# Two buffers for the residual rows of a conditioned transformer block, loaded and biased one block ahead, with a weight ring of eight

## The chip, the cores and the metric

The kernel runs on one core of one Trainium2 chip. The metric is the time of one execution in device microseconds (us); lower is better. All tensors are fp32. The engines that the text names are PE (TensorE, which multiplies matrices), DVE (VectorE), ACT (ScalarE), POOL (GpSimd) and SP (SyncE), whose queue issues nearly all transfers between the chip's main memory and the on-chip memory.

## The reference

The inputs are x with shape [8, 1024, 512], a condition vector [8, 512] and the weights of one block with 16 heads. Cut to what matters, this is computed:

```python
mod = silu(condition) @ Wada + bada
sh_a, sc_a, gt_a, sh_m, sc_m, gt_m = split(mod, 6, axis=1)
xm = layernorm(x, g1, be1) * (1 + sc_a[:, None]) + sh_a[:, None]
x = x + gt_a[:, None] * (causal_attention(xm, Wqkv) @ Wproj + bproj)
xm = layernorm(x, g2, be2) * (1 + sc_m[:, None]) + sh_m[:, None]
h = gelu(xm @ W1 + b1)
x = x + gt_m[:, None] * (h @ W2 + b2)
```

The gates multiply biases too: `gt_a * bproj` and `gt_m * b2` are the same for every token of a batch row, and the kernel adds each to the residual rows as one "bias row".

## The kernel before

The 8 x 1024 tokens are cut into 16 blocks of 512 tokens, two to a batch row; a block's tokens are four tiles of 128 rows. For each block the kernel projects k, q and v, attends, projects out (`proj`), normalizes again (`mt`), and runs the MLP as four up steps (`u`, L1058) and four down steps (`d`, L1107). The k, q, v, up and down products are one level of Strassen's scheme: seven products in place of eight, of operands that are sums of quarters. The sums of weights are made in the first blocks and kept in main memory.

The program is a fixed order of instructions, written by a planner in the kernel itself. It keeps a running estimate of each engine's time in `now`, and of when each value will have been written or released in `written` and `left`. Two streams are interleaved: attention (`attend`, L1743) and the linear work (`plan`, L231, a list of steps for each window). Window `w` holds what runs beside the attention of block `w`: late MLP steps of block `w - 2`, the projection and MLP of block `w - 1`, and the k, q and v of later blocks. Each step is a generator: it yields the values that it needs next, and `work` (L1343) advances the thread with the shortest wait. `start` (L1324) opens a side thread.

Weights come in pieces of 256 KB through a ring of `RING` buffers, in an order that is fixed ahead (`order`, L317). `fetch` (L328) issues the next piece's load on SP as soon as the planner has released a buffer, so in the SP queue the load of piece i + 9 stands right after the place at which piece i was last used, and it waits for PE to get there. SP issues in order. A transfer that has to wait holds up every load behind it.

Four other kinds of transfer stand in the same queue and matter here:

- `store` (L1100) writes a block's finished rows, in two halves. It is recorded right after the last additions to those rows were recorded, so SP waits there until POOL or DVE has done them.
- `load_xr` (L1258) fetches the residual rows of a block: four transfers of 256 KB. There is one buffer (`xrp`, L78), which the block before has to have stored first; block 14 alone borrows a buffer of k. The step stands in the window just ahead of `rows` and `proj`.
- `hat_a<-held_a` (L678) is the second half of a transposition of the next block's normalized input through main memory: four strided loads of 256 KB each.
- `gate_broadcasts` (L508) loads a gate row and a bias row for a batch row, each spread over 128 partitions.

`project_out` (L1006) multiplies the attention output with four pieces of Wproj for each of the four tiles, and POOL or DVE adds the bias row `gba` and the gated product to the residual rows. `down` (L1107) adds `gbm` at its first step. `either` (L150) picks POOL or DVE for such an addition by the planner's times.

Of the kernel before, what the change touches and what calls it, by code (L numbers as in the profile page):

```python
# [9 lines left out]
F32 = mybir.dt.float32  # L10
# [12 lines left out]
def kernel(  # L23
# [47 lines left out]
    HB = D // 2  # L71
    RING = 9

# [154 lines left out]
    def mlp_steps(n):  # L228
# [6 lines left out]
        0: [("load_xa", 2), ("preps",), ("k", 1), ("norm_a", 2), ("gates", "a"), ("q", 1)]  # L235
        + [("mod", 3), ("at", 2), ("v", 1), ("mod", 4), ("columns_m",), ("gates", "m")],
    }
    late = []
    for w in range(1, NB):
        n = w - 1  # L240
        m = mlp_steps(n)
        even = blocks[n][1] == 0
        rows_a = [("rows", blocks[n][0], "a")] if even else []
        rows_m = [("rows", blocks[n][0], "m")] if even else []
        own = m[:1] + ([("load_xa", w + 2)] if w + 2 < NB else []) + m[1:3]
        own += [("norm_a", w + 2)] if w + 2 < NB else []
        if w == NB - 1:
            steps = late[:1] + [("load_xr", n)] + rows_a + [("proj", n), ("mt", n)] + late[1:]
            steps += [("v", w)] + rows_m + own + m[3:6]
            late = m[6:]  # L250
        else:

            steps = late + [("v", w), ("load_xr", n)] + rows_a + [("proj", n), ("mt", n), ("k", w + 1)]
            if w == 2:
                steps = late + [("v", w), ("k", w + 1), ("load_xr", n)] + rows_a + [("proj", n), ("mt", n)]
            if w == 1:
                steps = [("load_xr", n)] + rows_a + [("k", w + 1), ("proj", n), ("mt", n)]
# [11 lines left out]
    plan[NB] = [("load_xr", n), late[0], ("beside", late[1]), ("proj", n), ("mt", n)] + mlp_steps(n)  # L269

# [126 lines left out]
    make_identity(nc, ident)  # L397
    mask = const.tile([P, 2 * P], F32, tag="mask", name="mask")
    for i in range(2):
        make_causal_mask(nc, mask[:, ts(i, P)], MASKED)  # L400
    eps = const.tile([P, 1], F32, tag="eps", name="eps")
    nc.gpsimd.memset(eps, EPS)
    ones = const.tile([P, P], F32, tag="ones", name="ones")
    nc.gpsimd.memset(ones, 1.0)
# [103 lines left out]
    def gate_broadcasts(b, kind):  # L508

        for name in (f"g{kind}", f"gb{kind}"):  # L510
            row = rowp.tile([P, D], F32, tag=f"row{name}", name=f"row_{name}_{b}")
            nc.sync.dma_start(row, kept_rows[name][b : b + 1, :].to_broadcast([P, D]))
            gate_rows[name] = row

# [476 lines left out]

    residual, stored = {}, {}
    y_count, y_keys = [0], {}
# [12 lines left out]
    def project_out(n):  # L1006
        at = take(NC)
        yield [("attended", n)], []
        attT = qTs[n]
        tiles = [residual[n][:, t, :] for t in range(NTT)]  # L1010
        for t, xt in enumerate(tiles):
            xt_job = lambda t=t, xt=xt: add_to(xt, gate_rows["gba"], [("row", "gba")], [("xr", n, t)])
            pool_jobs.append((xt_job, [("xr", n, t)]))
        last = n == NB - 1
# [38 lines left out]
        release(*at)  # L1053
        run_pool_jobs(True)
        if not last:
            normalize(residual[n], f"m{n}", [("xr", n, t) for t in range(NTT)])
# [35 lines left out]
    def settle(n, f, t, y, ky):  # L1092
# [5 lines left out]
        add_to(residual[n][:, half(t, 2), c], y, [ky], keys)  # L1098

    def store(n, t):  # L1100
        b, h = blocks[n]
        for i in (2 * t, 2 * t + 1):
            r0 = h * TB + i * P
            nc.sync.dma_start(out[b, r0 : r0 + P, :], residual[n][:, i, :])
        stored[n + 1] = max(stored.get(n + 1, 0.0), due([("xr", n, 2 * t), ("xr", n, 2 * t + 1)]))

    def down(n, part):  # L1107
# [85 lines left out]
        if part == 0:  # L1193
            yield [("g", n, 0), ("g", n, 1), "prepared"], []
            for i in range(NTT):
                add_to(residual[n][:, i, :], gate_rows["gbm"], [("row", "gbm")], [("xr", n, i)])
            combine(nc.vector, "B12", "B12", "B11")
# [47 lines left out]
    def perform(step):  # L1245
# [12 lines left out]
        elif kind == "load_xr":  # L1258
            n = step[1]
            b, h = blocks[n]  # L1260
            if n == NB - 2:
                xr = kvp.tile([P, NTT, D], F32, tag="kT", name=f"xr_{n}")
            else:
                xr = xrp.tile([P, NTT, D], F32, tag="xr", name=f"xr_{n}")
            residual[n] = xr
            for t in range(NTT):
                r0 = h * TB + t * P
                nc.sync.dma_start(xr[:, t, :], x[b, r0 : r0 + P, :])
                landed = max(now["PE"], stored.get(n, 0.0)) + LANDING + 700 * t
                written["xr", n, t] = landed  # L1270
        elif kind == "norm_a":
# [179 lines left out]
    def diagonals(parts, sc):  # L1451

        if parts[-1][4] == parts[0][4]:
            first, span = parts[0][3] - P, len(parts) * P
            return span, sc[:, :, first : first + span]
        return 2 * P, sc.rearrange("p j (a c) -> p j a c", c=2 * P)[:, :, :, P:]
# [19 lines left out]
    def scores_by_heads(n, g, parts, reads):  # L1476

        h = blocks[n][1]
        for some in (range(HPG - 1), range(HPG - 1, HPG)):
# [14 lines left out]
            for j, bank in of.items():  # L1494
                if parts[0][1] == h:
                    span, place = diagonals(parts, banks[bank].unsqueeze(1))
                    place = place[:, 0]
                    shape_of = mask[:, :span]
                    if len(place.shape) == 3:
                        shape_of = shape_of.rearrange("p (a c) -> p a c", c=P)  # L1500
                    nc.vector.tensor_tensor(place, place, shape_of, ALU.add)
# [8 lines left out]
    def scores_at_once(n, g, parts, reads):  # L1510
# [15 lines left out]
        if parts[0][1] == h:  # L1526
            span, place = diagonals(parts, sc)
            shape_of = mask[:, :span].unsqueeze(1)
            if len(place.shape) == 4:
                shape_of = shape_of.rearrange("p o (a c) -> p o a c", c=P)  # L1530
            nc.vector.tensor_tensor(place, place, shape_of.to_broadcast(place.shape), ALU.add)  # L1531
            note("DVE", 165 + 4.16 * span, ["st"])
# [127 lines left out]
    def finish(n, g):  # L1660
# [7 lines left out]
        for i, (c0, w, term, held) in enumerate(terms):  # L1668
            for j in range(HPG):
                r = slice(j * hd, (j + 1) * hd)  # L1670
                nc.tensor.matmul(  # L1671
                    banks[bank][r, TB - w :], ones[:, :hd], term[:, j, c0 : c0 + w],
                    start=i == 0, stop=i == len(terms) - 1, skip_group_check=True,
# [163 lines left out]
    for n in range(NB):  # L1837
        written["attended", n] = NEVER
        written["v done", n] = NEVER
        written["m used", n] = NEVER  # L1840
        if n > 1:
# [73 lines left out]
```

## Time and profile before

| what | value |
|---|---|
| median of 3 runs | 3567.45 us (3565.46 to 3569.86) |
| the profiled execution's own time | 3568.64 us |
| its span, first to last instruction | 3566.9 us |
| PE busy | 3490.9 us (98%) |
| DVE busy | 2181.1 us (61%) |
| POOL busy | 2081.8 us (58%) |
| ACT busy | 1186.3 us (33%) |
| moved by DMA | 461.77 MB, mean 129 GB/s |
| mean granted clock of TensorE | 0.995 |

The profile page gives the busy time of each engine, the chain of work that ended last, and groups of instructions. A row of a group ends with the engine's idle time just before these instructions and with what ended that idle time. The view of waits sums those idle times by who waited for whom; "SPq" there is SP's queue. The timeline lists instructions in order of time: start, length, engine, line, what is written and read, a count, and in brackets the idle time ahead of them with what ended it.

### The profile page before, as it was taken

The numbers are of one execution on the slowest core, as the hardware profiler recorded it, in microseconds if no ns is written. First come the engines' busy times: TensorE is split into PE (matmuls) and PEld (weight loads), VectorE is DVE, ScalarE is ACT, GpSimd is POOL, SyncE is SP. The second block draws the span as 40 slices with busy tenths as digits, with TensorE's granted clock in tenths as the row PEclk, the third lists the DMA queues.
The fourth block names the chain that finished last, engine by engine and source line by source line (L and its number), as shares of the span: only waits on it lengthen the run. The fifth ranks groups of instructions, "written<-read, shape, count | busy, mean of one in ns | idle before, by whom it ended". The sixth has DMA issues, their size and how long they took to land.

```text
span 3566.9 us, 120690 instructions
## 1 busy us (share of the span) xinstructions
PE 3490.9 (98%) x54621; PEld 1741.5 (49%) x54621; DVE 2181.1 (61%) x2395; ACT 1186.3 (33%) x1229; POOL 2081.8 (58%) x2247
## 2 busy tenths in 40 slices
PE   8999999999999999999999999999999999999999
PEld 4444445444554545445454454544545445454445
DVE  6776575665746557365574665746666466665663
ACT  2334333352323514234241442323423134231521
POOL 3667746675456754577536675366762667526660
PEclk9999999999999999999999999999999999999999
DMA  6753434435453344533445334453344533434334
GB/s 201 241 179 93 141 102 127 124 108 155 113 150 107 104 154 117 158 100 101 146 121 148 105 102 146 120 151 103 103 140 126 152 103 105 143 108 142 92 111 137
DMA packets 318259, 461.77 MB, mean 129 GB/s; under 512 B 27052, under 2 KB 177388, under 8 KB 315700
## 3 DMA queue, kind: packets, MB, share of 16 engines
q1 hardware_dynamic: 317632, 454.03, 43.4%
q8 instruction: 430, 7.05, 0.8%
q14 instruction: 81, 0.66, 0.1%
q10 hardware_dynamic: 116, 0.03, 0.0%
HBM read 408.80 MB, written 43.06 MB: 127 GB/s over the span
## 4 chain that ended last, share of the span: by engine, by line
PE 88%; DMA 4%; POOL 3%; DVE 3%; ACT 1%; issue 1%; SPq 1%; ACTq 0%; DVEq 0%; POOLq 0%
PE bank L202 60%; PE sc L1517 8%; PE po L1650 7%; PE st L1610 7%; PE st L1598 3%; DMA w<-in_L_cond_Wproj_dram 2%; PE bank L1671 2%; POOL pT L1740 1%; DMA hat_a<-held_a 1%; PE bank L728 1%; DVE mx L1534 1%; POOL hT L161 1%; PE bank L1572 0%; DVE sc L1531 0%; DMA w<-in_L_cond_Wada_dram 0%
## 5 line engine op out<-in xcount | busy, mean ns | idle before, releaser
L1740 POOL TENSOR_TENSOR pT<-pT,pT 128x256 f32<-128x256 f32 (+3 forms) x1254 | 1213.2, 1003 | 336.1 <-PE po L1650 183.4
L1622 ACT ACTIVATE pT<-st 128x2048 f32<-128x2048 f32 x288 | 541.0, 1878 | 1115.0 <-PE st L1610 1032.9
L202 PE MATMUL bank<-w,hT 128*32 128x256 f32 x14336 | 813.7, 380 | 0.2 <-POOL pT L1627 0.2
L1534 DVE TENSOR_REDUCE mx<-sc 128x4 f32<-128x2048 f32 (+3 forms) x384 | 666.0, 1755 | 216.2 <-PE sc L1517 210.0
L202 PEld LDWEIGHTS bank<-w,hT 128*32 128x32 f32 x14336 | 451.6, 110 | 367.6 <-issue 82.5
L202 PE MATMUL bank<-xm_m,w 128*32 128x256 f32 x8192 | 498.4, 380 | 0.0
L202 PE MATMUL bank<-t_m,w 128*32 128x256 f32 x6144 | 383.2, 380 | 0.1
L202 PEld LDWEIGHTS bank<-xm_m,w 128*32 128x32 f32 x8192 | 256.0, 110 | 222.2 <-issue 55.5
L1627 POOL TENSOR_SCALAR_AFFINE_SELECT pT<-pT 128x512 f32<-128x512 f32 x256 | 169.0, 678 | 332.4 <-ACT pT L1622 332.2
L1517 PE MATMUL sc<-kT,qT 32*128 32x512 f32 (+3 forms) x3072 | 329.1, 520 | 2.0 <-DVE mx L1534 1.7
L1531 DVE TENSOR_TENSOR sc<-sc,mask 128x1024 f32<-128x1024 f32 (+1 forms) x160 | 162.8, 1018 | 273.5 <-PE sc L1517 187.3
L1650 PE MATMUL po<-pT,v 128*32 128x512 f32 (+3 forms) x3048 | 303.1, 493 | 2.0 <-POOL pT L1627 2.0
L1610 PE MATMUL st<-qT,kT 32*128 32x512 f32 (+3 forms) x3072 | 300.6, 487 | 0.0
L202 PEld LDWEIGHTS bank<-t_m,w 128*32 128x32 f32 x6144 | 189.4, 110 | 180.7 <-issue 57.5
L202 PE MATMUL bank<-w,qT 128*32 128x512 f32 x2048 | 244.7, 606 | 21.2 <-DMA w<-in_L_cond_Wproj_dram 19.7
L1689 DVE RECIPROCAL rec<-rec 128x128 f32<-128x128 f32 x256 | 224.5, 919 | 33.2 <-ACT rec L1680 33.2
L202 PE MATMUL bank<-xm_a,w 128*32 128x256 f32 x3968 | 244.6, 380 | 0.0
L1517 PEld LDWEIGHTS sc<-kT,qT 32*128 32x128 f32 x3072 | 129.3, 183 | 172.8 <-ACT pT L1622 63.9
L202 PE MATMUL bank<-t_a,w 128*32 128x256 f32 x2944 | 190.9, 382 | 0.4 <-ACT xm_m L738 0.4
L193 DVE TENSOR_TENSOR hT<-bank,u_u 128x512 f32<-128x512 f32 x192 | 129.3, 685 | 101.2 <-PE bank L202 99.9
L1064 ACT ACTIVATE hT<-hT,cols 128x512 f32<-128x512 f32 x256 | 164.5, 711 | 55.3 <-DVE hT L193 54.7
L202 PEld LDWEIGHTS bank<-xm_a,w 128*32 128x32 f32 x3968 | 123.5, 110 | 106.5 <-issue 30.8
(216 smaller groups left out, 3396.6 us busy)
## 6 DMA issues: line engine op xcount, KB each, us to landing
w<-in_L_cond_W_dram SPq DMA_DIRECT2D x384, 256.0 KB
w<-kept_up_S SPq DMA_DIRECT2D x256, 256.0 KB
w<-kept_down_S SPq DMA_DIRECT2D x256, 256.0 KB
w<-kept_qkv_S SPq DMA_DIRECT2D x180, 256.0 KB
w<-in_L_cond_Wqkv_dram SPq DMA_DIRECT2D x147, 256.0 KB
hat_a<-in_x_dram SPq DMA_DIRECT2D x64, 256.0 KB
w<-in_L_cond_Wproj_dram SPq DMA_DIRECT2D x64, 256.0 KB
xr<-in_x_dram SPq DMA_DIRECT2D x64, 256.0 KB
```

The source lines that it names most:

```text
L193: nc.vector.tensor_tensor(out, src, other, op)
L202: nc.tensor.matmul(ps[r, :], columns, rhs, start=start, stop=stop, skip_group_check=True)
L1064: nc.scalar.activation(hT[:, i, :], hT[:, i, :], AF.Gelu, bias=cols[:, O_B1 + f : O_B1 + f + 1])
L1517: nc.tensor.matmul(sc[:, j, c0 : c0 + w], qTs[n][r, gg, ts(qt, P)], keys_of(n, kh)[r, gg, :w], start=True, stop=True, skip_group_check=True,)
L1531: nc.vector.tensor_tensor(place, place, shape_of.to_broadcast(place.shape), ALU.add)
L1534: nc.vector.tensor_reduce(maxima[n, gg][:, kh, qt, :], sc[:, :, c0 : c0 + w], axis=AX.X, op=ALU.max)
L1610: nc.tensor.matmul(st[:, j, c0 : c0 + w], kT[r, gg, ts(k % NTT, P)], qT[r, gg, TB - w :], start=False, stop=True, skip_group_check=True,)
L1622: nc.scalar.activation(pT[:, :, :used], st[:, :, :used], AF.Exp, scale=scale)
L1627: nc.gpsimd.affine_select(diagonal, diagonal, pattern=[[0, HPG], [1, P]], compare_op=ALU.is_ge, fill=0.0, base=0, channel_multiplier=-1,)
L1650: nc.tensor.matmul(po[r, TB - w :], v[:, k % NTT, g * P + j * hd : g * P + (j + 1) * hd], pT[:, j, c0 : c0 + w], start=(k == 0), stop=last ...
L1689: nc.vector.reciprocal(some, some)
L1740: nc.gpsimd.tensor_tensor(into, into, pT[:, j, c0 : c0 + w], ALU.add)
```

## The change

- The residual rows get two buffers. `load_xr` becomes a side thread: it waits until the planner thinks block `n - 2` is stored, issues the load as two transfers of 512 KB, waits until the planner has the additions to block `n - 1` that were recorded by then, loads the bias row, and hands the four bias additions to POOL's list of jobs. The step moves from just ahead of `proj` of block `n` to the MLP of block `n - 1`, between its first and second down step. `project_out` no longer adds the bias. Block 14 has a residual buffer like the others.
- The two bias rows share one buffer (`rowgb`). So each is loaded once per block, 16 times each, where each was loaded once per batch row, 8 times. `gbm` is loaded at the end of `project_out`.
- `store` becomes a side thread: it is recorded when the planner thinks the additions are done, and writes two tiles in one transfer.
- The weight ring goes from nine buffers to eight.
- The causal mask is kept for 128 columns and repeated by its access pattern; the tile of ones has 32 columns in place of 128.

```diff
-    RING = 9
+    RING = 8
-    xrp = ctx.enter_context(tc.tile_pool(name="xrp", bufs=1))
+    xrp = ctx.enter_context(tc.tile_pool(name="xrp", bufs=2))
...
-        + [("mod", 3), ("at", 2), ("v", 1), ("mod", 4), ("columns_m",), ("gates", "m")],
+        + [("mod", 3), ("at", 2), ("v", 1), ("load_xr", 0), ("mod", 4), ("columns_m",), ("gates", "m")],
...
-            steps = late + [("v", w), ("load_xr", n)] + rows_a + [("proj", n), ("mt", n), ("k", w + 1)]
+            steps = late + [("v", w)] + rows_a + [("proj", n), ("mt", n), ("k", w + 1)]
...
-                steps += m[3:5]
+                steps += m[3:5] + [("load_xr", w)]
...
-                steps += m[3:6] + at
+                steps += m[3:5] + [("load_xr", w)] + m[5:6] + at
...
+    def bias_row(n, kind):
+
+        b = blocks[n][0]
+        row = rowp.tile([P, D], F32, tag="rowgb", name=f"row_gb{kind}_{n}")
+        nc.sync.dma_start(row, kept_rows[f"gb{kind}"][b : b + 1, :].to_broadcast([P, D]))
+        gate_rows[f"gb{kind}"] = row
+        written["row", f"gb{kind}", n] = now["PE"] + LANDING
...
     def project_out(n):
         at = take(NC)
-        yield [("attended", n)], []
+        yield [("attended", n), ("xr begun", n)], []
...
-        for t, xt in enumerate(tiles):
-            xt_job = lambda t=t, xt=xt: add_to(xt, gate_rows["gba"], [("row", "gba")], [("xr", n, t)])
-            pool_jobs.append((xt_job, [("xr", n, t)]))
...
     def store(n, t):
-        b, h = blocks[n]
-        for i in (2 * t, 2 * t + 1):
-            r0 = h * TB + i * P
-            nc.sync.dma_start(out[b, r0 : r0 + P, :], residual[n][:, i, :])
-        stored[n + 1] = max(stored.get(n + 1, 0.0), due([("xr", n, 2 * t), ("xr", n, 2 * t + 1)]))
+        unstored.setdefault(n, 2)
+
+        def when_added():
+            yield [("xr", n, 2 * t), ("xr", n, 2 * t + 1)], []
+            nc.sync.dma_start(some_rows(out, n, t), residual[n][:, half(t, 2), :])
+            unstored[n] -= 1
+            if unstored[n] == 0:
+                written["stored", n] = now["PE"]
+
+        start(when_added())
+
+    def load_xr(n):
+
+        if n > 1:
+            yield [("stored", n - 2)], []
+        xr = xrp.tile([P, NTT, D], F32, tag="xr", name=f"xr_{n}")
+        residual[n] = xr
+        for t in range(2):
+            nc.sync.dma_start(xr[:, half(t, 2), :], some_rows(x, n, t))
+        for t in range(NTT):
+            written["xr", n, t] = now["PE"] + LANDING
+        if n > 0:
+            yield [("xr", n - 1, t) for t in range(NTT)], []
+        bias_row(n, "a")
+        row = ("row", "gba", n)
+        for t in range(NTT):
+            job = lambda t=t: add_to(xr[:, t, :], gate_rows["gba"], [row], [("xr", n, t)])
+            pool_jobs.append((job, [("xr", n, t), row]))
+        written["xr begun", n] = 0.0
...
-            yield [("g", n, 0), ("g", n, 1), "prepared"], []
+            yield [("g", n, 0), ("g", n, 1), "prepared", ("row", "gbm", n)], []
```

More of the change, by code (lines that the diff above doesn't have):

```diff
@@ L268 @@
     n = NB - 1
-    plan[NB] = [("load_xr", n), late[0], ("beside", late[1]), ("proj", n), ("mt", n)] + mlp_steps(n)
+    plan[NB] = [late[0], ("beside", late[1]), ("proj", n), ("mt", n)] + mlp_steps(n)
     kept_sums = {}
@@ L397 @@
     make_identity(nc, ident)
-    mask = const.tile([P, 2 * P], F32, tag="mask", name="mask")
-    for i in range(2):
-        make_causal_mask(nc, mask[:, ts(i, P)], MASKED)
+    mask = const.tile([P, P], F32, tag="mask", name="mask")
+    make_causal_mask(nc, mask, MASKED)
     eps = const.tile([P, 1], F32, tag="eps", name="eps")
     nc.gpsimd.memset(eps, EPS)
-    ones = const.tile([P, P], F32, tag="ones", name="ones")
+    ones = const.tile([P, hd], F32, tag="ones", name="ones")
     nc.gpsimd.memset(ones, 1.0)
@@ L1258, in perform @@
         elif kind == "load_xr":
[L1259 to L1270, printed above, removed]
+            start(load_xr(step[1]))
         elif kind == "norm_a":
@@ L1527, in scores_at_once @@
             span, place = diagonals(parts, sc)
-            shape_of = mask[:, :span].unsqueeze(1)
-            if len(place.shape) == 4:
-                shape_of = shape_of.rearrange("p o (a c) -> p o a c", c=P)
+            shape_of = mask.unsqueeze(1).unsqueeze(1)
             nc.vector.tensor_tensor(place, place, shape_of.to_broadcast(place.shape), ALU.add)
```

36 lines of the change are left out of this document (21 added, 15 removed).

## The prediction

> **What bounds the kernel now.** I read the page's busy times first, then the waits of PE, then the waits of SP's queue, then the timeline of a stage in which PE waits. The page's head:
>
> ```profile
> span 3566.9 us, 120690 instructions
> PE 3490.9 (98%) x54621; PEld 1741.5 (49%) x54621; DVE 2181.1 (61%) x2395; ACT 1186.3 (33%) x1229; POOL 2081.8 (58%) x2247
> ```
>
> PE sets the time: it idles for 3566.9 - 3490.9 = 76 us in all. The change removes no matrix product, so what it can win is mostly in that idle time. The waits of PE, longest first, cut to those that the change can reach, and those of SP:
>
> ```profile
> PE bank L202 <- DMA w<-in_L_cond_Wproj_dram: 19.7, 14, 3.1
> PE st L1598 <- DVE mx L1534: 10.1, 8, 3.0
> ...
> PE bank L202 <- DVE v L193: 5.2, 3, 2.1
> ```
>
> ```profile
> SPq L340 <- PE bank L202: 1441.0, 622, 16.9
> SPq L338 <- PE bank L202: 1043.4, 478, 7.6
> SPq L1104 <- POOL xr L161: 80.5, 23, 9.0
> ...
> SPq L1104 <- DVE xr L158: 24.8, 3, 11.2
> ...
> SPq L1268 <- DMA out_dram<-xr: 11.0, 10, 2.3
> ```
>
> PE waits 19.7 us for pieces of Wproj, in 14 places, and for no other piece after the start. SP mostly waits for PE to free a ring buffer, which is how a full ring looks. It also stands 105.3 us at the stores (L1104) until the rows are added, but only 11.0 us at the loads of xr. So the one residual buffer as such costs little; what could cost is the store that blocks the queue. One such stage in SP's queue, then on POOL and PE:
>
> ```profile
> 1707.56 2.05 SPq L340 DMA_DIRECT2D w<-kept_qkv_S  x2
> 1714.09 0.82 SPq L1104 DMA_DIRECT2D out_dram<-xr  x2
> 1715.00 2.10 SPq L340 DMA_DIRECT2D w<-kept_qkv_S  x1
> 1717.20 0.39 SPq L338 DMA_DIRECT2D w<-in_L_cond_Wqkv_dram  x1
> 1717.68 0.42 SPq L342 DMA_DIRECT2D w<-in_L_cond_Wproj_dram  x1
> 1718.19 1.80 SPq L678 DMA_DIRECT2D hat_a<-held_a  x4
> 1720.09 0.38 SPq L342 DMA_DIRECT2D w<-in_L_cond_Wproj_dram  x1
> 1720.57 1.61 SPq L1104 DMA_DIRECT2D out_dram<-xr  x2
> 1722.98 2.82 SPq L342 DMA_DIRECT2D w<-in_L_cond_Wproj_dram  x2
> ```
>
> ```profile
> 1712.78 1.28 POOL L161 TENSOR_TENSOR xr<-xr,p_d 128x512 f32<-128x512 f32 x1
> 1718.33 1.28 POOL L161 TENSOR_TENSOR xr<-xr,y_d 128x512 f32<-128x512 f32 x1
> ```
>
> ```profile
> 1705.81 10.33 PE L202 MATMUL bank<-w,hT 128*32 128x256 f32 x188
> 1715.95 1.91 PE L202 MATMUL bank<-w,xm_a 128*32 128x256 f32 x32
> 1717.68 1.91 PE L202 MATMUL bank<-w,t_a 128*32 128x256 f32 x32
> ...
> 1726.31 1.04 PE L202 MATMUL bank<-w,qT 128*32 128x512 f32 x8
> 1729.89 1.07 PE L202 MATMUL bank<-w,qT 128*32 128x512 f32 x8 [2.54 <-DMA w<-in_L_cond_Wproj_dram]
> 1731.82 2.47 PE L202 MATMUL bank<-w,qT 128*32 128x512 f32 x12 [0.86 <-DMA w<-in_L_cond_Wproj_dram]
> ```
>
> SP issues nothing from 1709.6 to 1714.09: it waits for POOL's addition, which ends at 1714.06. That delays the strided loads hat_a to 1718.19. The second Wproj piece stands behind them and reaches PE only at 1729.89, 11.7 us after hat_a's first issue; PE has lost 2.54 us. The third piece follows with two 256 KB stores between them: 1731.82 - 1729.89 = 1.93 us for three transfers, 0.64 us for each. The stage loses 3.40 us.
>
> **The change, part by part.** I made the sum against the profiled execution, 3568.64 us, which is 1.2 us above the median; the difference is then taken from the median, 3567.45.
>
> *Stores once due, and the ring of eight, in the projection stages.* These have one answer together. In the changed program's order the first store of this stage stands four places later, behind the load that waits for the third of the last four down pieces; hat_a stands right behind that store. A piece is 1.73 us of PE (1717.68 - 1715.95). The down pieces end at 1705.81 + 10.33 = 1716.14, the third at 1714.41. The addition is done at 1714.06, so the store waits for nothing. With one load (0.39 us) and one store (0.41 us) ahead, hat_a is issued at about 1715.3, 2.9 us sooner. But a ring of eight releases each load one piece later, and now all four Wproj pieces stand behind hat_a, the first one too, which PE wants at 1726.31. The same distance in another stage, with the wait it ends in DVE and in PE:
>
> ```profile
> 2162.31 3.08 SPq L678 DMA_DIRECT2D hat_a<-held_a  x4
> ```
>
> ```profile
> 2171.79 1.92 PE L202 MATMUL bank<-w,qT 128*32 128x512 f32 x16 [1.79 <-DMA w<-in_L_cond_Wproj_dram]
> 2175.69 2.61 PE L202 MATMUL bank<-w,t_a 128*32 128x256 f32 x24 [1.98 <-DVE v L193]
> ```
>
> ```profile
> 2171.36 0.55 DVE L732 TENSOR_SCALAR xm_a<-hat_a,gaina,shifta 128x512 f32<-128x512 f32 x1 [5.72 <-DMA hat_a<-held_a]
> 2174.95 1.28 DVE L193 TENSOR_TENSOR v<-bank,u_v 128x512 f32<-128x512 f32 x2
> ```
>
> Here it is 2171.79 - 2162.31 = 9.5 us. Between 9.5 and 11.7 I take 11.0, nearer to the first stage, since as much weight and store traffic stands right ahead of hat_a. The first piece then arrives at 1726.3, as it is wanted. The third one stands behind the second and behind a store of 512 KB, four steps of 0.64 = 2.6 us after the first; PE wants it 1.73 us after. That leaves 0.9 us of stall in place of 3.40; with 11.7 it is 0.7 + 0.9 = 1.6, with 9.5 none. Six stages have this order in the changed program. One has the first store behind hat_a, 1.3 us more: I take 2.0 (0 to 2.5). Three have one Wproj piece ahead of hat_a: the same 2.6 - 1.73 between second and third, about 1.0 (0 to 1.5). One has two ahead (0.3, up to 1), one all four (none). Sum after: 6 x 0.9 + 2.0 + 3 x 1.0 + 0.3 = 10.7 in place of 19.7, so -9.0; the ends are 0 (-19.7) and 6 x 1.6 + 2.5 + 4.5 + 1 = 17.6 (-2.1).
>
> *What DVE does behind hat_a.* DVE works in order; at 2171.36 it had waited 5.72 us for hat_a, and the result v, for which PE then waits 1.98 us, came behind that. With hat_a some 3 us sooner most of these 5.2 us go: -4.2 (0 to -5.2). Next late for v is the product that it is made of, which PE has just run.
>
> *The loads of xr and the bias rows.* 64 loads become 32 of twice the size; 16 broadcasts of 256 KB become 32. Per block 1 MB leaves the place behind Wproj and comes, with 256 KB of bias row, into the first down steps: five times 256 KB at 0.64, 3.2 us. Ring pieces there have no wait in PE's list, and their cover is the ring itself: seven pieces of 1.73 = 12.1 us, less the few us of a load. I cost it at nothing; if the cover were gone it would be 16 x 3.2 = 51 us, an end that I leave out because PE has no wait there in 16 blocks now. Block 0 is tighter:
>
> ```profile
> 134.78 3.43 SPq L678 DMA_DIRECT2D hat_a<-held_a  x4
> ...
> 145.20 0.34 SPq L775 DMA_DIRECT2D kept_up_S<-prep_up  x1
> 145.63 0.93 SPq L338 DMA_DIRECT2D w<-in_L_cond_Wqkv_dram  x2
> ```
>
> The 1.25 MB now go ahead of this hat_a, and the loads at 145.63 come as the queue is full. +2 us (-1 to +4): half of the 3.2 us, as SP waits there until 145.20 anyhow. What is queued behind the new bias load is the next down pieces; it waits for four additions of the block before, which the planner has put ahead of it, so a wait of one or two additions at most, within those 12 us.
>
> *The 64 bias additions.* They stay 64, on POOL or DVE, but in the MLP:
>
> ```profile
> L161 POOL TENSOR_TENSOR xr<-xr,row_gba x35: 1257/1281/1738, 176.7 to 3437.4; 128x512 f32<-128x512 f32 x35
> ...
> L158 DVE TENSOR_TENSOR xr<-xr,row_gba x29: 677/682/1770, 465.7 to 3244.2; 128x512 f32<-128x512 f32 x29
> ```
>
> ```profile
> L158 DVE TENSOR_TENSOR xr<-xr,row_gbm x21: 675/1210/3579, 302.6 to 3367.1; 128x512 f32<-128x512 f32 x21
> ```
>
> Durations are min/median/max in ns. The same addition takes DVE 682 ns in the projection and 1210 ns in the MLP (the gbm row), so 29 of them cost 29 x 0.53 = 15 us more of DVE. DVE is 61% busy, so I cost it at nothing; without cover it is +15. [...]
>
> *Smaller parts.* The next group's transpositions on PE are placed sooner and more broken up:
>
> ```profile
> L728 PE MATMUL bank<-ident,hat_m 128*128 128x128 f32 x256 | 44.0, 295 | 4.5 <-ACT hat_m L651 3.4 <-ACT hat_m L624 1.0
> ```
>
> In the two programs' orders they stand in 66 separate runs before and in 75 after, so 18 more changes between them and the products. Each costs between nothing and one such instruction's length of 295 ns (0 to 5.3); I take something below the middle, +2.2 us. The mask's and the ones' shapes keep the elements per instruction: nothing, and DVE would hide it.
>
> The sum: -9.0 - 4.2 + 2.0 + 2.2 = -9.0 us. From the profiled execution 3559.6; from the median 3567.45 - 9.0 = 3558.5 us.
>
> **The rivals.** *A. The queue is held as before* (slower). If POOL's additions end later in fact than in the plan, hat_a goes out at 1718.2 as now, and all four pieces are behind it. The first then takes the second's place, 1729.89, against 1726.31: 3.6 + 0.9 = 4.5 us in place of 3.40, some +1 us in each of 12 stages, +12; with +4.2 from the start and the transposes and no gain on DVE: 3584. Each us by which hat_a is later costs each of the 12 stages about one, so the 9.0 us of the first part are gone at 9.0 / 12 = 0.75 us after the 1715.3 worked out above. For it speaks the ring's lost piece, which is certain; against it the 0.35 us by which the addition is early at 1714.06.
>
> *B. The transfer is the limit anyway* (no change). Stalls stay at their upper end, 17.6, and DVE's wait stays: -2.1 + 4.2 = +2, 3569. For it speaks that hat_a's 9.5 to 11.7 us remain, and a store of 512 KB now stands undivided ahead of the third piece.
>
> *C. Contention in the MLP* (slower). The +15 us of DVE come on the path of the scores, for which PE already waits 10.1 us (L1598 behind L1534): 3558.5 + 15 = 3574. Against it: 39% of DVE's time is free.
>
> *D. The change does not do what it says.* If the load of xr or the bias row waits in the new place for a store or an addition, SP stands in the MLP and not in the projection; with 12 us of cover nothing is lost and the main case holds, so it has no price of its own.
>
> **How the numbers follow.** The forecast has 0.48, by itself 3550 to 3567 (the sum's ends, not all at once); A 0.18, B 0.22, C 0.09, and 0.03 for a larger gain near the end at which all Wproj and DVE waits go, 3567.45 - 24.9 = 3542.6. About 0.2% (7.1 us) is what a measurement here can tell from no change: that is 3560.3, near the forecast. So 0.40 of the main case and the larger gain count as faster, 0.43; 0.08 of the main case and 0.16 of B as the same, 0.24; the rest of B, A and C as slower, 0.33. The range 3546 to 3582 leaves out about half of A and the larger gain.
>
> **What would show it.** Right: PE's wait for Wproj falls from 19.7 to about 11 us; the waits of SP at the stores fall from 105 us to under 40; hat_a is issued about 11 us ahead of the first Wproj product; DVE's and ACT's waits for hat_a shrink; the additions of gba stand in the MLP. Wrong: Wproj waits above 20 us (A, B), new PE waits for other ring pieces (the ring is too short), or more PE idle time behind DVE's maxima (C).

## The result, and the profile after

| | before | changed |
|---|---|---|
| median | 3568.65 us (3565.46 to 3571.1, 4 runs) | 3542.81 us (3541.91 to 3547.21, 4 runs) |
| ratio, 95% interval | | 0.9931 [0.9913, 0.9948] |
| profiled execution | 3568.64 us | 3542.2 us |
| its span | 3566.9 us | 3540.5 us |
| mean granted clock of TensorE | 0.995 | 0.998 |

The change makes the kernel about 26 us faster. The forecast was 3558.5 us, with a range from 3546 to 3582: the sign is right, the gain is almost three times as large as forecast, and the time lies 3 us below the range. The changed kernel was run again later on another chip: there it gains 20 us (3563.7 to 3543.55, ratio 0.9943).

The page's head of the changed kernel (span; then busy time, share and instructions of each engine):

```profile
span 3540.5 us, 120499 instructions
...
PE 3482.5 (98%) x54621; PEld 1738.0 (49%) x54621; DVE 2174.2 (61%) x2383; ACT 1190.1 (34%) x1237; POOL 2074.9 (59%) x2249
```

PE's idle time fell from 76.0 to 58.0 us (3540.5 - 3482.5), 18.0 us. The other 8.4 us of the 26.4 are PE's busy time, 3490.9 to 3482.5, with the same 54,621 products. The forecast had no gain of the second kind.

The waits of PE in the changed kernel (total, times, longest, in us):

```profile
PE st L1620 <- DVE mx L1556: 7.4, 6, 2.4
PE bank L202 <- DMA w<-in_L_cond_Wproj_dram: 7.2, 9, 1.5
```

The wait for Wproj fell from 19.7 to 7.2 us. The 5.2 us behind DVE's `v` are gone from the list, and the wait for the maxima of the scores fell from 10.1 to 7.4 us. One wait is new, for a piece of Wada in block 0:

```profile
151.20 0.60 PE L494 MATMUL bank<-w,condT 128*8 128x256 f32 x2 [2.66 <-DMA w<-in_L_cond_Wada_dram]
```

The waits of ACT and DVE for hat_a, first in the kernel before and then in the changed one, and SP's waits at the stores in the changed one:

```profile
ACT xm_a L738 <- DMA hat_a<-held_a: 72.8, 12, 10.6
...
DVE xm_a L732 <- DMA hat_a<-held_a: 53.4, 12, 6.0
```

```profile
ACT xm_a L745 <- DMA hat_a<-held_a: 45.5, 11, 6.0
...
DVE xm_a L739 <- DMA hat_a<-held_a: 22.0, 12, 3.2
```

```profile
SPq L1118 <- POOL xr L161: 15.8, 12, 6.7
...
SPq L1118 <- DVE xr L158: 5.0, 2, 3.4
```

ACT and DVE wait 67.5 us for hat_a in place of 126.2, and SP stands 20.8 us at the stores in place of 105.3. The stage that the prediction followed, in the timeline of the changed kernel:

```profile
1710.72 1.28 POOL L161 TENSOR_TENSOR xr<-xr,p_d 128x512 f32<-128x512 f32 x1
1711.70 0.38 SPq L338 DMA_DIRECT2D w<-in_L_cond_Wqkv_dram  x1
1712.18 0.42 SPq L1118 DMA_DIRECT2D out_dram<-xr  x1
1712.70 3.60 SPq L685 DMA_DIRECT2D hat_a<-held_a  x4
...
1716.39 0.85 SPq L342 DMA_DIRECT2D w<-in_L_cond_Wproj_dram  x2
1717.34 0.39 SPq L1118 DMA_DIRECT2D out_dram<-xr  x1
1717.82 1.48 SPq L342 DMA_DIRECT2D w<-in_L_cond_Wproj_dram  x2
...
1723.54 1.90 PE L202 MATMUL bank<-w,qT 128*32 128x512 f32 x16
...
1726.20 1.92 PE L202 MATMUL bank<-w,qT 128*32 128x512 f32 x16 [0.75 <-DMA w<-in_L_cond_Wproj_dram]
```

The addition ends at 1712.00 and the store behind it waits for nothing. hat_a goes out at 1712.70, 10.84 us ahead of the first Wproj product at 1723.54; before, it was 1726.31 - 1718.19 = 8.12 us. The stage loses 0.75 us at its third piece, where before it lost 3.40.

Where the 8.4 us of busy time come from is seen in a table of short stretches. The columns are the stretch, its length, the busy time of PE, PEld, DVE, ACT and POOL with their instructions, the granted clock, the share of the DMA engines and GB/s. First the kernel before, then the changed kernel, in the same stage:

```profile
1725.00:1730.00 5.00, 2.46 (x40) 1.02 (x36) 0.78 (x2) 1.08 (x2) 0.00 (x0) 1.00 1.05 305
1730.00:1735.00 5.00, 4.14 (x28) 0.91 (x31) 3.05 (x5) 1.15 (x2) 1.78 (x1) 0.72 0.96 320
1735.00:1740.00 5.00, 5.00 (x72) 2.08 (x68) 1.38 (x2) 0.00 (x0) 1.48 (x2) 0.94 0.50 177
```

```profile
1725.00:1730.00 5.00, 4.25 (x59) 1.71 (x56) 3.23 (x6) 0.00 (x0) 2.84 (x2) 1.00 0.48 163
1730.00:1735.00 5.00, 5.00 (x72) 2.10 (x68) 0.61 (x1) 1.30 (x1) 2.76 (x4) 1.00 0.16 52
1735.00:1740.00 5.00, 5.00 (x52) 1.31 (x44) 3.46 (x4) 0.57 (x1) 5.00 (x9) 1.00 0.02 3
```

Before, the granted clock falls to 0.72 and 0.94 in the ten us after the stall: 5 x 0.28 + 5 x 0.06 = 1.7 us of PE lost while it counts as busy. In the trace's record of the clock this is one stretch at 0.5, from 1732.2, 3.4 us long. There are four such places in the projection stages of the kernel before (1732.2, 1943.8, 2175.9 and, 6.8 us long, 2824.5), each in or right behind a stage that lost 3.3 to 3.9 us. Half of their length is 8.5 us, 7.8 us of it while PE was busy. In the changed kernel there is none in those stages. Counted where PE is busy, the half clock cost 14.6 us over the span before and 6.2 us after; what is left lies at the start and at the end. The difference is 8.4 us, all that PE's busy time lost: 3490.9 - 14.6 and 3482.5 - 6.2 are both 3476.3 us.

This much holds for the two profiled executions. The share that the clock has in the gain changes from one execution to the next. The record has the mean granted clock of 37 other executions of the kernel before, on three chips: from 0.995 to 0.999, 0.9967 on average. The two at 0.999 took 3556.1 and 3556.9 us, the four at 0.995 took 3568.6 to 3571.4 us, and 0.004 of 3565 us is 14 us: most of the spread of this kernel's time goes with the clock. The eight executions of the changed kernel average 0.9974. Estimated from these two averages, 0.0007 of 3565 us, the clock is worth 2 to 3 us of the gain in an average execution. The 18.0 us of idle time are the larger part; on the other chip, 20 us less these 2 to 3 leaves about as much.

The gain comes in steps. Worked out from the same product with a weight piece in both traces, it is 0.3 us at 838 us, 2.1 at 1490, 6.9 at 1924, 12.2 at 2153, 17.0 at 2364, 20.0 at 2798, 25.0 at 3043 and 26.4 us at the end, in time of the kernel before. The first 1500 us, where the stalls before were short, gained almost nothing.

### The profile page after: what moved, and what is told of

The parts are those of the page before. It is cut to its first block, busy times and chain, and to the rows that moved or that the text cites. A ratio compares the mean times of both kernels' runs of the same rounds, so it can differ in the third digit from the quotient of the medians.

```text
span 3540.5 us, 120499 instructions
## 1 busy us (share of the span) xinstructions
PE 3482.5 (98%) x54621; PEld 1738.0 (49%) x54621; DVE 2174.2 (61%) x2383; ACT 1190.1 (34%) x1237; POOL 2074.9 (59%) x2249
## 3 DMA queue, kind: packets, MB, share of 16 engines
q1 hardware_dynamic: 318928, 458.22, 42.9%
## 4 chain that ended last, share of the span: by engine, by line
PE 88%; DMA 4%; DVE 3%; POOL 2%; issue 1%; ACT 1%; SPq 0%; ACTq 0%; DVEq 0%; POOLq 0%
PE bank L202 61%; PE sc L1541 8%; PE po L1672 7%; PE st L1632 7%; PE st L1620 3%; DMA w<-in_L_cond_Wproj_dram 2%; PE bank L1693 2%; PE bank L735 1%; DVE mx L1556 1%; POOL pT L1762 1%; DMA w<-in_L_cond_Wada_dram 1%; PE bank L1594 0%; POOL hT L161 0%; POOL xr L161 0%; DVE sc L1553 0%
```

## The experiments

Two theories were to be told apart. The queue theory: the stores no longer hold up SP's queue, so that hat_a and the Wproj pieces behind it go out sooner, the stalls shrink below what half clock follows on, and that is the gain. The early-rows theory: the gain comes from the second residual buffer, since loads and bias additions leave the projection stage. (A third, that any rearrangement of the order would do, is tried only in so far as the same part was put in alone and taken out alone.) Kernels under one heading ran on the same chip, with runs of the kernel before beside them, to which the ratios refer. PE idle, PE busy and the waits are of one profiled execution each; "lost" is the time lost at half clock while PE was busy, worked out from the clock record of the trace. Without it, PE's busy time is 3473 to 3480 us in all 13 profiles, where with it it is 3479 to 3510.

| kernel | median us (range) | ratio [95%] | PE idle | PE busy | Wproj wait | SP at stores | lost |
|---|---|---|---|---|---|---|---|
| before | 3568.65 | 1 | 76.0 | 3490.9 | 19.7 | 105.3 | 14.6 |
| changed | 3542.81 | 0.9931 | 58.0 | 3482.5 | 7.2 | 20.8 | 6.2 |
| e_stores_due | 3542.97 (3540.32 to 3547.36) | 0.9947 [0.9932, 0.9962] | 61.1 | 3484.5 | 4.0 | 9.7 | 9.6 |
| e_ring8 | 3572.64 (3568.43 to 3577.3) | 1.0022 [1.0013, 1.0031] | 75.4 | 3491.5 | 26.7 | 104.1 | 16.4 |
| e_store_at_once | 3594.1 (3591.82 to 3598.07) | 1.0091 [1.0076, 1.0106] | 91.0 | 3503.0 | 38.2 | 108.2 | 26.9 |
| e_xr_late | 3550.43 (3548.53 to 3554.11) | 0.9962 [0.9949, 0.9974] | 64.3 | 3488.1 | 10.0 | 11.5 | 9.9 |
| e_changed | 3543.55 (3538.21 to 3544.63) | 0.9943 [0.9929, 0.9958] | 58.0 | 3483.4 | 11.1 | 21.1 | 8.1 |
| e_hold6 | 3532.06 (3531.75 to 3535.49) | 0.9916 [0.9901, 0.9931] | 49.9 | 3480.7 | 4.0 | 25.5 | 6.5 |
| e_hat_more | 3613.74 (3612.82 to 3615.1) | 1.0144 [1.0129, 1.0159] | 100.9 | 3510.2 | 43.4 | 15.5 | 35.6 |
| e_due_ring8 | 3550.48 (3545.49 to 3552.99) | 0.9963 [0.995, 0.9976] | 68.1 | 3479.3 | 13.1 | 8.2 | 3.4 |
| e_before_hold6 | 3566.27 (3557.18 to 3575.36) | 1.0007 [0.9994, 1.0021] | 70.6 | 3491.7 | 15.9 | 105.2 | 11.8 |
| e_due_hold6 | 3538.01 (3536.65 to 3541.94) | 0.9927 [0.9911, 0.9943] | 55.9 | 3484.3 | none | 16.8 | 11.2 |
| e_hold4 | 3532.59 (3528.21 to 3533.25) | 0.9907 [0.9892, 0.9923] | 50.2 | 3481.3 | 3.5 | 24.3 | 8.0 |

### One part of the change alone, and one part undone

**The stores once due, alone** (e_stores_due): the kernel before, ring of nine, one residual buffer, the load of the rows at its old place and the bias row as before. Since the store is now recorded later, the load of the rows waits for it as a side thread.

```diff
     def store(n, t):
-        b, h = blocks[n]
-        for i in (2 * t, 2 * t + 1):
...
+        def when_added():
+            yield [("xr", n, 2 * t), ("xr", n, 2 * t + 1)], []
...
+        start(when_added())
```

> The kernel before with one part of the change: stores recorded once the planner thinks the additions done (two transfers of 256 KB each), ring of nine, one residual buffer, bias rows and additions where they were. Theory Q (the stores no longer hold SP's queue, so hat_a and Wproj come sooner, PE waits no stretch long enough to lose its clock): nearly the whole gain, 3538 to 3550 us, PE's waits for Wproj under 10 us, granted clock 0.997 or more. Rival R (the gain is in the residual rows and bias additions being ready before the projection): no change, 3563 to 3572 us. Rival P (a chance rearrangement of the order): anything between.

It has the whole gain, as far as these runs tell: 0.9947 [0.9932, 0.9962], against 0.9931 [0.9913, 0.9948] and 0.9943 [0.9929, 0.9958] for the changed kernel on two chips. Its waits of PE for Wproj, and of SP at the stores:

```profile
PE bank L202 <- DMA w<-in_L_cond_Wproj_dram: 4.0, 7, 1.4
```

```profile
SPq L1108 <- POOL xr L161: 4.9, 6, 1.3
...
SPq L1108 <- DVE xr L158: 4.8, 3, 2.9
```

With the store out of the way of hat_a, the Wproj wait falls from 19.7 to 4.0 us, lower than in the changed kernel.

**The ring of eight alone** (e_ring8):

```diff
-    RING = 9
+    RING = 8
```

> The kernel before with a ring of eight and nothing else. Theory Q: each Wproj piece is issued one piece (1.73 us) later behind the same blocked queue, so its waits grow from 19.7 us to some 30 us and more stages lose the clock: slower, 3575 to 3595 us. Rival R: the ring has slack, no change, 3563 to 3572 us.

PE's wait for Wproj:

```profile
PE bank L202 <- DMA w<-in_L_cond_Wproj_dram: 26.7, 19, 3.1
```

It is 7 us more than before. By itself the smaller ring costs 0.22% [0.13, 0.31], about 8 us, less than the first theory expected and more than the second. The two profiled executions don't show it, 75.4 us idle against 76.0. The clock of all executions shows most of it: it averages 0.9951 against 0.9965 of the kernel before on that chip, which is about 5 us.

**The stores recorded at once, all else as changed** (e_store_at_once):

```diff
-        def when_added():
-            yield [("xr", n, 2 * t), ("xr", n, 2 * t + 1)], []
...
-        start(when_added())
+        nc.sync.dma_start(some_rows(out, n, t), residual[n][:, half(t, 2), :])
+        unstored[n] -= 1
```

> The changed kernel with one part undone: the stores (still by pairs of tiles) are recorded at once, so SP stands there until the rows are added. Theory Q: the gain goes and the shorter ring is left, 3565 to 3590 us, PE's waits for Wproj 20 us or more, clock 0.995 or less. Rival R: the gain stays, 3540 to 3548 us.

The waits of PE for Wproj, and of SP at the stores:

```profile
PE bank L202 <- DMA w<-in_L_cond_Wproj_dram: 38.2, 18, 4.8
```

```profile
SPq L1116 <- POOL xr L161: 87.3, 21, 9.1
```

This is the prediction's rival A, and it is slower than the kernel before by 0.91% [0.76, 1.06]: SP stands 108.2 us at the stores, all four Wproj pieces stand behind hat_a in seven of the twelve stages, and half clock costs 26.9 us. The time lies above both expectations. Without this one part the change is a loss, two buffers and all.

**The rows loaded late, all else as changed** (e_xr_late): the load of the rows and the bias row go back to just ahead of `proj`.

```diff
-            steps = late + [("v", w)] + rows_a + [("proj", n), ("mt", n), ("k", w + 1)]
+            steps = late + [("v", w), ("load_xr", n)] + rows_a + [("proj", n), ("mt", n), ("k", w + 1)]
...
-                steps += m[3:5] + [("load_xr", w)]
+                steps += m[3:5]
```

> The changed kernel with one part undone: the residual rows and their bias row are loaded just ahead of the projection as before (two buffers and everything else as changed), so the bias additions fall into the projection again. Theory Q: no change against the changed kernel, 3539 to 3549 us. Rival R: the gain goes, 3560 us or more.

The waits of PE, and those of SP at the bias row:

```profile
PE st L1620 <- DVE mx L1556: 10.8, 10, 2.7
PE bank L202 <- DMA w<-in_L_cond_Wproj_dram: 10.0, 13, 1.6
```

```profile
SPq L518 <- DVE xr L158: 40.2, 14, 6.4
...
SPq L518 <- POOL xr L161: 26.2, 11, 2.5
```

It is still 0.38% faster than the kernel before, 0.9962 [0.9949, 0.9974]. The time lies between the two expectations, and this run isn't a clean one: the bias rows share a buffer, so at the late place the row's load (L518) waits 66.4 us in SP's queue for additions. Still it shows what the early place is good for: the wait for the score maxima is 10.8 us as in the kernel before (10.1), while it is 7.4 with the additions in the MLP.

### The ring once the queue is free, a dose of stall, and a smaller wait

**The changed kernel again** (e_changed), as it was, for the three that follow.

> The changed kernel itself, once more beside the kernel before and the three that follow, as their reference. All theories: about 26 us below the kernel before (ratio about 0.993), PE's wait for Wproj about 7 us, and about 8 us of PE time lost at half clock.

3543.55 us, 0.9943 [0.9929, 0.9958]: 20 us below the kernel before, not the 26 expected. The kernel before is at a better clock here, 0.9970 on average against 0.9975 of these four, so the clock is worth about 2 us of the 20. PE's idle time is 58.0 us as in the first profile. The Wproj wait was 11.1 us in this profile, 7.2 in the first: it differs by some 4 us between these two executions.

**Stores once due with a ring of eight** (e_due_ring8): e_stores_due with `RING = 8`. (In both, a half of the rows is still two transfers of 256 KB, not the one that the expectation tells of.)

> The kernel before with its stores recorded once due and halves written in one transfer each, as in the earlier run with these two alone, but with a ring of eight in place of nine; one residual buffer, the bias row as before. If the ring of eight costs nothing once the queue is free, as the changed kernel suggests, it is within 3 us of the run with nine (ratio about 0.995 to the kernel before). If the ring's one piece (1.7 us of PE) is what the Wproj pieces lack, PE's wait for Wproj rises from 4.0 us to 12 to 20 us and the time by 10 to 20 us: ratio 0.998 to 1.001.

PE's wait for Wproj:

```profile
PE bank L202 <- DMA w<-in_L_cond_Wproj_dram: 13.1, 13, 1.7
```

The wait rises from 4.0 to 13.1 us, as the second theory had it, but the longest is 1.7 us, no stretch at half clock lies between 460 and 3390 us, and the ratio goes only from 0.9947 to 0.9963 [0.995, 0.9976], between the two expectations. On the same chip the changed kernel is 7 us faster, and the ranges don't touch (3538.21 to 3544.63 against 3545.49 to 3552.99). So with a ring of eight the rest of the change (the two buffers, the early rows and the larger transfers) is worth about 7 us, and the lost ring piece costs about as much. The two nearly cancel.

**A dose of stall** (e_hat_more): the changed kernel, with two of the four strided loads issued twice.

```diff
-        for m in range(NTT):
+        for m in (0, 1, 0, 1, 2, 3):
             some = held[:, ts(m, D)].rearrange("(a i) d -> i a d", i=Q)
```

> The changed kernel, with two of the four strided hat_a loads issued twice (six loads of 256 KB in place of four), so that each Wproj piece behind them lands later by about 2.2 us, worked out from 1.1 us for each of the two (8.2 to 10.1 us for the four is the upper end, 2.5 us for each). A dose of stall put back without any other part of the change. Theory that a stall costs its own length only: PE's wait for Wproj goes from 7 to about 30 us, PE's busy time stays at 3482.5 us, and the time is 20 to 25 us above the changed kernel. Theory that stalls of 2 us and more also bring the half clock: the same rise of the wait and, on top, PE busy 8 to 20 us longer (lost clock from 8 to 16 to 28 us), 30 to 45 us above the changed kernel.

The page's head, then the waits of PE for Wproj and of SP at the strided loads:

```profile
span 3611.1 us, 120533 instructions
...
PE 3510.2 (97%) x54621; PEld 1750.3 (48%) x54621; DVE 2169.6 (60%) x2383; ACT 1190.0 (33%) x1237; POOL 2070.5 (57%) x2249
```

```profile
PE bank L202 <- DMA w<-in_L_cond_Wproj_dram: 43.4, 12, 4.9
```

```profile
SPq L685 <- DMA hat_a<-held_a: 70.0, 27, 6.4
```

The dose was larger than worked out: the second load into the same rows waits in SP's queue until the first has landed, 70.0 us in all, so the pieces behind came about 6 us later a stage and not 2.2. Both expectations of the total, 20 to 25 and 30 to 45 us over the changed kernel, are therefore too low; it is 70. What the run tells apart is untouched by that. PE's idle time rose by 42.9 us over the changed kernel on the same chip (58.0 to 100.9), and its busy time, for the same products, by 26.8 us (3483.4 to 3510.2); the two make the span's 69.7 us. By the clock record 27.5 us more of its busy time was lost at half clock (35.6 against 8.1). One stage of it, in stretches of 5 us (columns as above):

```profile
1755.00:1760.00 5.00, 1.09 (x21) 0.39 (x12) 0.09 (x1) 0.12 (x1) 0.00 (x0) 0.89 0.92 244
1760.00:1765.00 5.00, 4.71 (x24) 1.35 (x28) 3.74 (x6) 2.11 (x3) 1.78 (x1) 0.50 0.93 336
```

So a stall costs more than its length: here 26.8 / 42.9 = 0.6 us of slow clock for each us of idle time.

**A smaller wait ahead of hat_a** (e_hold6): the changed kernel, in which the planner lets 6000 ns in place of 8000 pass between the write of held_a and hat_a.

```diff
-        written["turned", key] = now["PE"] + HOLDING
+        written["turned", key] = now["PE"] + 10000
...
-    HOLDING = 8000
+    HOLDING = 6000
```

The first line keeps the planner's time for the landing of hat_a where it was, 16000 ns after the write.

> The changed kernel, with the planner's wait between the writing of the normalized input and its strided loads cut from 8000 to 6000 ns, so that hat_a goes out about 2 us sooner in each projection stage. If the queue's order of hat_a ahead of the Wproj pieces is all that is left of the stalls, PE's wait for Wproj falls from 7.2 us to below 2 us, the half clock stays away as in the changed kernel, and the time is 3534 to 3540 us, 3 to 8 us below the changed kernel. If the loads then wait in SP's queue for the transfers that write held_a, the stalls stay or grow: 3543 to 3560 us, with SP or hat_a waiting on held_a.

PE's waits:

```profile
PE st L1620 <- DVE mx L1556: 5.6, 5, 2.4
...
PE bank L202 <- DMA w<-in_L_cond_Wproj_dram: 4.0, 7, 0.8
```

3532.06 us, 0.9916 [0.9901, 0.9931], and 11.5 us faster than the changed kernel beside it, with ranges that don't touch. The time is below both expectations. The Wproj wait was to fall below 2 us and fell to 4.0 (from 11.1), no longer than 0.8 us at a time. The rest of the gain is 1.9 us of the wait for maxima and 2.7 us of PE's busy time.

### Is it the queue or the planner's wait?

**The smaller wait in the kernel before** (e_before_hold6), the same edit and nothing else.

> The kernel before with the planner's wait ahead of hat_a cut from 8000 to 6000 ns and nothing else, the edit that made the changed kernel faster by about 11 us. In the SP queue hat_a now stands one or two pieces earlier, in nine of the stages still right behind a store that waits for POOL's addition. If that store is what holds hat_a, the loads go out as before or under 1 us sooner, SP's wait at the stores stays above 80 us, PE's wait for Wproj stays at 12 to 25 us, and the time is 3556 to 3572 us, ratio 0.997 to 1.002. If the planner's wait alone is what makes hat_a late, PE's wait for Wproj falls to 4 to 8 us, the half clock goes, and the ratio is 0.990 to 0.994, so that the change would not have been needed.

The timeline of the stage that was followed above:

```profile
1717.23 2.05 SPq L340 DMA_DIRECT2D w<-kept_qkv_S  x2
...
1722.44 1.28 POOL L161 TENSOR_TENSOR xr<-xr,p_d 128x512 f32<-128x512 f32 x1
...
1723.76 0.82 SPq L1104 DMA_DIRECT2D out_dram<-xr  x2
...
1726.84 1.83 SPq L678 DMA_DIRECT2D hat_a<-held_a  x4
```

The ratio is 1.0007 [0.9994, 1.0021]. SP still stands at the store, from 1719.3 until POOL's addition ends at 1723.7, and hat_a comes behind it, 1.0 us sooner against the products than in the kernel before. SP's waits at the stores stay at 105.2 us. In each of the twelve stages from 600 us on, SP stands 4.5 us or more at a store ahead of hat_a. Against the first Wproj product hat_a goes out 0.1 to 1.3 us sooner in nine of them and 4.4 to 5.1 us sooner in the other three; there all four Wproj pieces now stand behind it, and 1.0 to 1.5 us of stall is left. The edit that wins 11 us in the changed kernel wins nothing here, and in nine of the twelve stages hat_a goes out little sooner, since it still stands behind the store. This is a strong sign for the queue theory.

**Stores once due and the smaller wait, ring of nine, one buffer** (e_due_hold6).

> The kernel before with the stores recorded once due, the ring of nine and one residual buffer, and in addition the planner's wait ahead of hat_a cut from 8000 to 6000 ns. If what is left of the stalls is the place of hat_a in the queue, and the second residual buffer adds nothing once the stores are out of the way, this is as fast as the changed kernel with the shorter wait (3532 us, ratio 0.989 to 0.993) with PE's wait for Wproj below 3 us. If the early loads of the residual rows matter in their own right, it is 5 to 10 us slower than that: 0.993 to 0.995.

0.9927 [0.9911, 0.9943]. PE has no wait for Wproj left, yet it is some 5 us slower than the changed kernel with a smaller wait on the same chip (below; 3536.65 to 3541.94 against 3528.21 to 3533.25). Neither expectation holds fully: the ratio fits the first, the difference to its neighbour the second. One line of PE's waits accounts for most of it:

```profile
PE st L1612 <- DVE mx L1548: 12.4, 11, 3.7
```

That wait is 5.8 us in e_hold4:

```profile
PE st L1620 <- DVE mx L1556: 5.8, 5, 2.4
```

In all runs with the bias additions in the projection stage it is 10.0 to 15.3 us; with the additions in the MLP it is 5.6 to 7.5, but for the two runs with long Wproj stalls (11.0 and 10.7).

**Smaller still** (e_hold4): the changed kernel with 4000 ns (and 12000 for "turned").

> The changed kernel with the planner's wait ahead of hat_a at 4000 ns in place of 8000 (6000 gave 3532 us). At 6000 the loads already waited in SP's queue for the transfers that write held_a, 5.5 us in all. If that is the floor, the loads go out no sooner, SP waits 15 to 30 us at them, nothing behind them is late since Wproj is wanted later, and the time is 3528 to 3534 us. If the wait in the queue holds up the loads of other pieces, PE's waits for other ring pieces appear and it is 3536 to 3550 us.

SP's wait at the strided loads:

```profile
SPq L685 <- DMA held_a<-xm_a: 18.9, 10, 2.8
```

3532.59 us, 0.9907 [0.9892, 0.9923]: not to be told from 6000 ns, with 3.5 us of Wproj wait. The loads now wait 18.9 us in the queue for held_a to be written, so little more can be won there. The changed kernel with either smaller wait beats both kernels of this case, by about 32 us the one before and by about 11 us the changed one.

## Why the prediction was wrong

**What was right.** The mechanism in the queue, and the steps of the stage that was worked out. hat_a was to go out 2.9 us sooner against the products; it was 10.84 - 8.12 = 2.7. It was to be issued 11.0 us ahead of the first Wproj product; it was 10.84. The stall was to go from 3.40 to 0.9 us and to move to the third piece, behind the large store; it is 0.75, at the third piece. SP's waits at the stores were to fall below 40 us; they are 20.8.

**The step that failed** is the first sentence of the argument, that what the change "can win is mostly in that idle time", and the sum built on it, in which every stall is counted by its length alone. Of the 26.4 us of the profiled executions 8.4 are PE's busy time: stalls of 2 us and more were often followed by a stretch at half clock that PE spends busy (37 of 48 such places in the 13 profiles), and the kernel before paid 7.8 us for that in its projection stages. The sum had no term for it. The number was on the page, a mean granted clock of 0.995: half a per cent of 3567 us is 18 us, a quarter of PE's idle time, and it was not asked where that lay. A table of short stretches around the stall that was quoted, as shown above, would have told.

The clock is only about half of what was missed, and less in an average execution (2 to 3 us, as worked out above). The other half is in the idle time itself. The terms for it came to -9.0 - 4.2 + 2.0 = -11.2 us, and it fell by 18.0: the Wproj term was too small, and a gain of 2.7 us at the score maxima had been put at nothing. So even with a term for the clock the forecast gain would have been too small.

**The terms, forecast and measured.**

| term | forecast | measured | |
|---|---|---|---|
| Wproj wait | -9.0 (-19.7 to -2.1) | -12.5; -8.6 in the second profile | in its ends |
| wait behind DVE's v | -4.2 | -5.2 | all of it |
| block 0 | +2.0 (-1 to +4) | +2.7, the new wait at 151.2 us; +1.1 in the second profile | right |
| transposes on PE | +2.2 (0 to +5.3) | +2.0 in their own row; PE's busy time as a whole shows none | not shown |
| bias additions in the MLP | 0 (+15 without cover) | score maxima -2.7 | other sign |
| granted clock | no term | -8.4 in this pair of executions | left out |

The other waits of the first 460 us shrank, so that at 460 us the changed kernel is 0.5 us behind. The row for the transposes (their busy time was 44.0 us before):

```profile
L735 PE MATMUL bank<-ident,hat_m 128*128 128x128 f32 x256 | 46.0, 297 | 3.6 <-ACT hat_m L658 3.6
```

Apart from the half clock, PE's busy time is 3476.3 us in both kernels, so these 2.0 us don't add to the span. The terms measured make -12.5 - 5.2 + 2.7 - 2.7 - 8.4 = -26.1; the span fell by 26.4, so -0.3 us is spread over small waits.

**The rivals.** A (the queue is held) did not come about, but e_store_at_once shows that it was no fancy: +0.91%, about 30 us (3594.1 against 3564.6 on that chip) where the forecast had +16.5; here, too, the half clock was left out, which cost 12.3 us more in its profile than in that of the kernel before (26.9 against 14.6). Its distance was small, too: the addition in this stage ended 0.18 us before the store was issued. B (the transfer is the limit) fell: the Wproj pieces came sooner. C (contention in the MLP) was right about the engine and wrong about the time. The additions of gba on DVE did become slow:

```profile
L158 DVE TENSOR_TENSOR xr<-xr,row_gba x36: 681/1665/1774, 441.8 to 3217.2; 128x512 f32<-128x512 f32 x36
```

The median is 1665 ns where it was 682; what slows them there was not shown. But they left the place where DVE is wanted for the score maxima, and that wait got shorter, not longer; e_xr_late, with the additions back in the projection (10.8 us), shows the same from the other side. D had no price and needed none. The case that was given 0.03, all Wproj and DVE waits gone, gives 3542.6 us, by chance the time that was measured: 7.2 us of Wproj wait stayed, and the clock and the score maxima made up for it.

**What the change as a whole is.** One of its parts, the stores recorded once due, brings by itself as much as the whole. The rest, the second buffer with its early rows above all, is worth about 7 us with a ring of eight, and the ring's lost piece costs 6 to 8. Whether the second buffer with a ring of nine would gain another 7 us was not tried.

## What to carry to other kernels

In a queue that issues in order, an instruction that waits for an engine is paid for by every load behind it (SP stood 105.3 us at the stores in the kernel before and 20.8 us in the changed one, and PE's wait for Wproj went from 19.7 to 7.2 us): look at who stands behind a waiting store, and record the store when its data is due. A stall of PE is to be priced by its length and by what the granted clock does after it (0.6 us of slow clock for each us of idle time in e_hat_more), which differs from one execution to the next (its mean from 0.995 to 0.999 in the kernel before), so read the clock in stretches of a few us around the stalls whenever its mean is below 1. Shorten the long stalls first: in the projection stages here, nine waits of at most 1.5 us cost their 7.2 us, and four stages that each lost 3.3 to 3.9 us cost 7.8 us beside that.

## What the runs showed of the hardware

Half clock followed stalls of little more than 2 us. For the 13 profiles of this case, between 460 and 3390 us, I summed PE's idle times that lie within 4 us of each other and looked whether a stretch at 0.5 begins within 7 us of their end.

| idle time in one place | places | followed by half clock |
|---|---|---|
| 1.5 to 2.0 us | 19 | 0 |
| 2.0 to 3.0 us | 18 | 10 |
| 3.0 to 4.0 us | 19 | 16 |
| over 4.0 us | 11 | 11 |

Each such stretch was 3.4 or 6.8 us long, so it cost at most 1.7 or 3.4 us. Single stalls of 2.0 to 2.4 us brought one (2.04 us in e_hold6, 2.24 and 2.37 in e_xr_late), with PE busy on both sides.

The length of a stall alone does not tell whether half clock follows. In the kernel before, one stall of 2.15 us that ends at 2823.4 us is followed by it at 2824.5, while the stage at 2382.9 us lost 3.33 us, in stalls of 1.26 and 2.07 us, and the one at 2625.3 us lost 2.95 us in a single stall, and both kept their clock (granted 1.00 from 2382 to 2397 and from 2620 to 2640).
